# Loading two weight blocks by chunks of 32 rows into 128 partitions instead of by partition blocks of 32

## The chip, the cores and the metric

The kernel runs on one core of a Trainium2 chip. Its time is the device time of one execution, in microseconds (us). The engines are TensorE (PE; its weight loads are PEld), VectorE (DVE), ScalarE (ACT), GpSimd (POOL) and SyncE (SP). SP computes nothing here: it issues transfers, and ACT issues a few as well. All transfers are carried by the core's 16 DMA engines.

## The reference, cut to what matters

```python
h = jnp.maximum(_layernorm(x, axis=-1), 0.0)            # x: 128 graphs x 128 nodes x 768
q = _split_heads(h @ Wq + bq)                           # W: 768 x 768, 12 heads of 64
k = _split_heads(h @ Wk + bk)
v = _split_heads(h @ Wv + bv)
scores = jnp.einsum('bhqd,bhkd->bhqk', q, k) / 8 + beta * adj[:, None]
scores = jnp.where(adj[:, None] > 0, scores, -9e15)
out = x + (softmax(scores) @ v)                         # heads side by side again
```

Everything is float32.

## The kernel before, in words

The 128 graphs are worked on in 32 groups (G) of four (GRP). For each group three slices of projections are made: "qk0" (columns 0 to 383 of Wq and Wk), "v" (all of Wv) and "qk1" (columns 384 to 767 of Wq and Wk). The order is qk0, v, qk1, and the attention of a group is woven into the slices that follow.

From group 1 on, a slice is computed with sums of weight blocks (the tiles T_qk and T_v) in place of the weights themselves, line 557 (`product_z`). These sums are made once, during group 0, by DVE and POOL (`prepare`, lines 281 to 304): 45 of them, of which 11 stay in SBUF (names res_...) and 34 are written to HBM (names kept_..., line 290) and read back for each group (line 339). A sum that is to be written to HBM is built in a tile named prep_..., of which there are five, and three more shared with the attention's tile "e"; the next sum in the same tile can begin when the store has landed.

Group 0 uses the raw weights. They lie in one large tile, sbig: the first RAW = 4608 elements of a partition hold Wq and Wk of qk0 (later those of qk1), the next 4608 hold Wv, and behind them lie the first rows of x, an identity and some constants. Each weight matrix has 768 rows, and the row that goes with partition p and chunk c (c = 0 to 5) is 192 a + 32 c + j, where p = 32 a + j; a = 0 to 3 is a block of 32 partitions. The matmuls of group 0 take two chunks at a time: step k = 0, 1, 2 of a product uses chunks 2k and 2k + 1.

The opening of the program runs as follows.

- Four transfers bring the first two graphs of x (line 204), two from SP and two from ACT.
- `raw_qk0(k)` brings chunks 2k and 2k + 1 of Wq and Wk: for k = 0 Wq from SP and Wk from ACT, then k = 1 from SP. `load_x(0, 1)` brings the other two graphs of group 0, in four transfers. Then come k = 2 and `raw_v()`, all from SP.
- Behind them SP issues bv_b (the bias of v for all partitions, line 876), adj of group 0 (line 488), x of group 1 (line 196, eight transfers), and then the stores of the prepared sums (line 290).
- PE starts with fillers and transposes (lines 927, 913) and then computes qk0 for the first two graphs (`first_row`, line 1065), in the order: k = 0 for graph 0, k = 0 for graph 1, k = 1, k = 2. Then follow qk0 for the other two graphs (`plain_slice`, line 849), the v slice (line 849; the bias is added by a matmul with bv_b, line 854, behind k = 0 of each of its six products) and qk1.

The instructions of each engine and of each queue run in the order of the program. Each transfer counts up one of eight semaphores, taken in turn, and before a transfer is issued its queue waits for the one that used the same semaphore before it. So a queue has to wait for the landing of the transfer eight places earlier, counted over both queues.

One transfer elsewhere in the kernel has a source of the kind that the change introduces: `block` is filled in all 128 partitions from a small table of 32 rows in HBM that is read four times (lines 438 and 439). It happens once per group from group 2 on.

```python
later(lambda: nc.sync.dma_start(to.rearrange("p b s g -> p (b s g)"),
                                turned.rearrange("i b s -> i (b s)")[None].to_broadcast([NB, SQ, NB * 2 * GRP])), then)
```

Of the kernel before, what the change touches and what calls it, by code (L numbers as in the profile page):

```python
# [17 lines left out]
P = 128  # L18
# [12 lines left out]
@with_exitstack  # L31
def kernel(
    ctx: ExitStack,
    tc: tile.TileContext,
    x: bass.AP,
    adj: bass.AP,
    wq: bass.AP,
    bq: bass.AP,
    wk: bass.AP,
    bk: bass.AP,  # L40
    wv: bass.AP,
    bv: bass.AP,
    beta: bass.AP,
    out: bass.AP,
):

    nc = tc.nc
    keep = ctx.enter_context(tc.tile_pool(name="keep", bufs=1))
    bad = keep.tile([1, 1], I32, name="bad")
    args = (x, adj, wq, bq, wk, bk, wv, bv, beta, out)
    direct(tc, *args, bad)
    again = nc.values_load(bad[0:1, 0:1])
    with tc.If(again > 0):
        general(tc, *args)
# [69 lines left out]
def direct(ctx, tc, x, adj, wq, bq, wk, bk, wv, bv, beta, out, bad):  # L129
# [10 lines left out]
    nc = tc.nc  # L140
    B, N, D = x.shape
    HD = D // HEADS
    NC = D // P
# [6 lines left out]
    SQ = 32  # L150
    NB = P // SQ
# [21 lines left out]
    def flat(lo, hi):  # L173
        return sbig[:, lo:hi]
# [25 lines left out]
    for g in range(2):  # L200
        t = xg[0, g]
# [19 lines left out]

    wt = {}

    rows_of = {}
    for name, w in (("q", wq), ("k", wk), ("v", wv)):
        rows_of[name] = w.rearrange("(a c j) n -> a j c n", a=NB, j=SQ)

    def name_raw(u, v):
        for k in range(3):
# [2 lines left out]

    qk0_raw = flat(0, RAW).rearrange("p (c i j n) -> p c i j n", c=NC, i=2, j=3)

    def load_rows(engine, t, name, cols, chunks, order=range(NB)):
        for a in order:
            engine.dma_start(t[a * SQ:(a + 1) * SQ], rows_of[name][a][:, chunks, cols])

    def raw_qk0(k, engines=(nc.sync, nc.sync)):

        c = slice(2 * k, 2 * k + 2)
        for i, name in enumerate(("q", "k")):
            load_rows(engines[i], qk0_raw[:, c, i].rearrange("p c j n -> p c (j n)"), name, slice(0, 3 * P), c,
                      ((0, 1, 2, 3), (2, 3, 0, 1))[i])

    def raw_qk1_piece(at):
        v = flat(0, RAW).rearrange("p (c i n) -> p c i n", c=NC, i=2)
# [4 lines left out]

    def raw_v():
        t = flat(RAW, 2 * RAW).rearrange("p (c n) -> p c n", c=NC)
        load_rows(nc.sync, t, "v", slice(0, D), slice(0, NC))
        for k in range(3):
            for j in range(3):
                wt["v", f"B{k}{j}"] = t[:, 2 * k:2 * k + 2, j * 2 * P:(j + 1) * 2 * P].rearrange("p c (i n) -> p c i n", i=2)
# [75 lines left out]
    def load_T():  # L334
        if nt[0] < len(ring):
# [3 lines left out]
            nc.sync.dma_start(t, kept[sl, n])  # L339

    raw_qk0(0, (nc.sync, nc.scalar))
    raw_qk0(1)
    load_x(0, 1)
    raw_qk0(2)
    name_raw(0, qk0_raw)

# [526 lines left out]


    raw_v()
    nc.sync.dma_start(bv_b, bv[None, :].to_broadcast([P, D]))
    turned[0, "raw"] = load_adj(0)
# [455 lines left out]
```

## Time and profile before

| what | value |
|---|---|
| time, median of 3 runs (lowest to highest) | 2679.64 us (2677.68 to 2682.68) |
| the profiled execution: its own time | 2679.08 us |
| its span, from the first to the last instruction | 2677.2 us |
| granted TensorE clock | 0.998 |
| PE busy | 2652.1 us, 99% of the span |
| DVE, POOL, ACT busy | 81%, 77%, 65% |
| DMA: moved, mean rate | 721.70 MB, 270 GB/s |

The span is cut by the profile into rows of several views. In the timeline a row gives the start in us, the time taken, the engine ("SPq" and "ACTq" are the queues that issue transfers), the line of the kernel, and what is written from what, and in brackets the idle time before it with what ended it. In a table by windows, the columns are the busy time of each engine, the granted clock, the mean busy share of the 16 DMA engines and the GB/s that they moved; the share can go a little above 1. Durations come from the profiled execution, whose own time is 0.56 us under the median of the runs, less than the runs differ among themselves.

### The profile page before, as it was taken

What the parts mean: (1) busy time and instruction counts of PE and PEld (TensorE: products, weight loads), DVE (VectorE), ACT (ScalarE), POOL (GpSimd) and SP (SyncE); (2) the same over time, 40 slices, a digit from 0 to 9 for tenths busy, and PEclk for the clock granted to TensorE, in tenths of its full rate; (3) what the DMA queues carried; (4) which work ended last, traced back from release to release, by engine and by line L of the source; (5) the groups of instructions that cost most, each with busy time, mean ns of one, the idle gap of its engine ahead of it and who ended that gap; (6) DMA issues with size and microseconds to landing.
All of it is one profiled execution on the core that took longest, in us unless ns stands there. A gap on an engine that the chain in (4) does not pass through costs nothing.

```text
span 2677.2 us, 121501 instructions
## 1 busy us (share of the span) xinstructions
PE 2652.1 (99%) x52041; PEld 2563.4 (96%) x52041; DVE 2179.3 (81%) x2701; ACT 1747.9 (65%) x4608; POOL 2070.9 (77%) x3043
## 2 busy tenths in 40 slices
PE   9999999999999999999999999999999999999998
PEld 8799999999999999999999999999999999999997
DVE  7877888778888778888788887788887888887885
ACT  2567766676666677666766666776667676667654
POOL 5877778877778777788777787777887777887774
PEclk9999999999999999999999999999999999999999
DMA  8889888889888998889898888988898988898875
GB/s 252 270 273 282 272 268 277 270 269 282 277 271 272 266 287 265 276 275 277 265 282 279 269 273 273 283 272 272 276 280 264 280 278 271 274 278 272 260 239 159
DMA packets 526436, 721.70 MB, mean 270 GB/s; under 512 B 105916, under 2 KB 370120, under 8 KB 525896
## 3 DMA queue, kind: packets, MB, share of 16 engines
q1 hardware_dynamic: 525248, 713.12, 86.5%
q8 instruction: 411, 6.73, 1.0%
q14 instruction: 129, 1.06, 0.1%
q10 hardware_dynamic: 648, 0.79, 0.1%
HBM read 647.73 MB, written 66.05 MB: 267 GB/s over the span
## 4 chain that ended last, share of the span: by engine, by line
PE 39%; POOL 33%; ACT 13%; issue 6%; DMA 4%; DVE 4%; SPq 0%; POOLq 0%; ACTq 0%; DVEq 0%
PE pair L557 33%; POOL v L614 4%; PE pair L693 4%; POOL A L479 3%; POOL v L613 3%; POOL home L612 3%; PE pair L636 3%; ACT x L448 3%; ACT e L646 3%; POOL home L599 2%; POOL home L601 2%; ACT home L575 2%; ACT home L577 2%; POOL v L610 2%; POOL home L611 2%
## 5 line engine op out<-in xcount | busy, mean ns | idle before, releaser
L581 DVE TENSOR_TENSOR home<-home,pair 128x896 f32<-128x896 f32 x810 | 860.8, 1076 | 274.1 <-PE pair L557 217.4
L557 PE MATMUL pair<-sbig,T_qk 128*64 128x128 f32 x13020 | 832.9, 273 | 1.7 <-DVE sbig L474 0.8
L557 PEld LDWEIGHTS pair<-sbig,T_qk 128*64 128x64 f32 x13020 | 708.4, 137 | 11.4 <-issue 6.6
L557 PE MATMUL pair<-A,T_qk 128*64 128x128 f32 x6944 | 465.3, 273 | 0.0
L599 POOL TENSOR_TENSOR home<-home 128x256 f32<-128x256 f32 x298 | 246.6, 827 | 269.2 <-DVE home L581 261.6
L676 ACT ACTIVATE e<-e,sm 128x64 f32<-128x64 f32 x1512 | 382.3, 347 | 108.7 <-DVE sm L664 108.7
L557 PE MATMUL pair<-T_v,sbig 128*64 128x128 f32 x6944 | 415.4, 274 | 0.0
L693 PE MATMUL pair<-v,e 128*64 128x65 f32 x6048 | 401.6, 221 | 5.8 <-DVE e L644 5.7
L575 ACT ACTIVATE home<-pair 128x640 f32<-128x640 f32 x325 | 232.3, 715 | 262.4 <-PE pair L557 201.8
L557 PEld LDWEIGHTS pair<-T_v,sbig 128*64 128x64 f32 x6944 | 380.9, 137 | 12.3 <-issue 10.5
L557 PEld LDWEIGHTS pair<-A,T_qk 128*64 128x64 f32 x6944 | 377.4, 137 | 4.8 <-ACT e L705 4.4
L693 PEld LDWEIGHTS pair<-v,e 128*64 128x64 f32 x6048 | 356.2, 137 | 15.8 <-DVE e L644 12.8
L557 PE MATMUL pair<-sbig,res_qk 128*64 128x128 f32 x4340 | 288.4, 273 | 0.0
L602 POOL TENSOR_TENSOR home<-home 128x256 f32<-128x256 f32 x298 | 239.1, 802 | 23.4
L600 POOL TENSOR_TENSOR home<-home 128x256 f32<-128x256 f32 x298 | 229.2, 769 | 23.4
L557 PEld LDWEIGHTS pair<-sbig,res_qk 128*64 128x64 f32 x4340 | 234.6, 137 | 5.3 <-issue 5.3
L703 ACT ACTIVATE sm<-pair,tiny 128x8 f32<-128x8 f32 x189 | 49.5, 262 | 284.8 <-PE pair L693 284.7
L448 ACT ACTIVATE x<-x,block 128x192 f32<-128x192 f32 x480 | 232.6, 556 | 0.0
L601 POOL TENSOR_TENSOR home<-home 128x128 f32<-128x128 f32 x298 | 213.2, 715 | 23.4
L644 DVE SCALAR_TENSOR_TENSOR e<-pair,biasT 128x1024 f32<-128x1024 f32 x189 | 225.2, 1216 | 4.6 <-PE pair L636 4.6
L646 ACT ACTIVATE e<-e 128x1024 f32<-128x1024 f32 x189 | 194.0, 1068 | 52.6 <-DVE e L644 48.6
L479 POOL TENSOR_TENSOR A<-A 128x256 f32<-128x256 f32 x186 | 169.2, 910 | 57.0 <-DVE A L469 57.0
(204 smaller groups left out, 4595.7 us busy)
## 6 DMA issues: line engine op xcount, KB each, us to landing
T_qk<-kept_qk SPq DMA_DIRECT2D x713, 448.0 KB, 5.0
T_v<-kept_v SPq DMA_DIRECT2D x341, 448.0 KB, 4.3
xo<-in_x_dram SPq DMA_DIRECT2D x189, 256.0 KB, 5.0
out_dram<-xo SPq DMA_DIRECT2D x189, 256.0 KB, 6.2
x<-in_x_dram SPq DMA_DIRECT2D x248, 192.0 KB, 6.5
sbig<-in_x_dram SPq DMA_DIRECT2D x116, 384.0 KB, 6.4
kept_qk<-prep_qk SPq DMA_DIRECT2D x23, 448.0 KB, 3.3
adj<-in_adj_dram SPq DMA_DIRECT2D x128, 64.0 KB, 3.0
```

Of the source, the lines that this page charges most:

```text
L448: nc.scalar.activation(t, t, AF.Relu, bias=shift[G, n], scale=rstd[G, n])
L479: e.tensor_tensor(t[:, 0:2], t[:, 7:8].to_broadcast([P, 2, P]), t[:, 5:7], ALU.subtract)
L557: nc.tensor.matmul(p[q:q + HD, at, :], lhs[:, q:q + HD], rhs, start=(first and at % 4 == 0), stop=True, skip_group_check=True)
L575: nc.scalar.activation(t[:, 0:5], p[:, 0:5], AF.Copy, scale=float(sign))
L581: nc.vector.tensor_tensor(t, t, p[:, 0:7], op)
L599: e.tensor_tensor(t[:, 1:4:2], t[:, 1:4:2], twice(5), ALU.add)
L600: e.tensor_tensor(t[:, 2:5:2], t[:, 2:5:2], twice(1), ALU.add)
L601: e.tensor_tensor(t[:, 4], t[:, 4], t[:, 6], ALU.add)
L602: e.tensor_tensor(t[:, 0:7:6], t[:, 0:7:6], twice(2), ALU.add)
L646: trailing.append(lambda: nc.scalar.activation(e, e, AF.Exp, scale=1.0 / ISCALE))
L676: nc.scalar.activation(o[:, r, b, 0:HD], pa[:, r, b, 0:HD], AF.Copy, scale=t[:, 1, r, b:b + 1])
L693: nc.tensor.matmul(pa[q:q + HD, 2 * g + i, :], k[:, q:q + HD], vt[G, "v", r, h // 4][:, 4 * g + h % 4, :], start=True, stop=True, skip_gro ...
```

## The change

Each transfer now carries one chunk into all 128 partitions, where it carried two chunks (for Wv six) into 32 partitions. For qk0, 24 transfers of 96 KB become 12 of 192 KB; for v, 4 of 576 KB become 6 of 384 KB. The rows that are copied, their length (1536 B for qk0, 3072 B for v) and their places in sbig are the same. The source of a transfer was a list of 32 rows by two (six) chunks, and is now a list of 4 blocks by 32 rows; the destination was 32 partitions, and is now 128.

```diff
-    rows_of = {}
+    rows_of, whole_of = {}, {}
     for name, w in (("q", wq), ("k", wk), ("v", wv)):
-        rows_of[name] = w.rearrange("(a c j) n -> a j c n", a=NB, j=SQ)
+        whole_of[name] = rows_of[name] = w.rearrange("(a c j) n -> a j c n", a=NB, j=SQ)
...
-    def load_rows(engine, t, name, cols, chunks, order=range(NB)):
-        for a in order:
-            engine.dma_start(t[a * SQ:(a + 1) * SQ], rows_of[name][a][:, chunks, cols])
+    def load_chunk(engine, t, name, cols, c):
+        engine.dma_start(t, whole_of[name][:, :, c, cols])
 
     def raw_qk0(k, engines=(nc.sync, nc.sync)):
 
-        c = slice(2 * k, 2 * k + 2)
-        for i, name in enumerate(("q", "k")):
-            load_rows(engines[i], qk0_raw[:, c, i].rearrange("p c j n -> p c (j n)"), name, slice(0, 3 * P), c,
-                      ((0, 1, 2, 3), (2, 3, 0, 1))[i])
+        for c in (2 * k, 2 * k + 1):
+            for i, name in enumerate(("q", "k")):
+                load_chunk(engines[i], qk0_raw[:, c, i].rearrange("p j n -> p (j n)"), name, slice(0, 3 * P), c)
...
     def raw_v():
         t = flat(RAW, 2 * RAW).rearrange("p (c n) -> p c n", c=NC)
-        load_rows(nc.sync, t, "v", slice(0, D), slice(0, NC))
+        for c in range(NC):
+            load_chunk(nc.sync, t[:, c], "v", slice(0, D), c)
```

On PE the order of the instructions does not change. On SP, the opening of the queue stood as follows (partitions x chunks x elements; DMAHW0 to DMAHW7 are the eight semaphores):

```order
L204 DMA sbig<-in_x_dram 64x768 x2
L237 DMA sbig<-in_L_gnn_Wq_dram 32x2x384 x8
L237 DMA sbig<-in_L_gnn_Wk_dram 32x2x384 x4
L196 DMA x_1_129<-in_x_dram 32x8x192 x4
L237 DMA sbig<-in_L_gnn_Wq_dram 32x2x384 x4
L237 DMA sbig<-in_L_gnn_Wk_dram 32x2x384 x4
L237 DMA sbig<-in_L_gnn_Wv_dram 32x6x768 x4
L876 DMA bv_b<-in_L_gnn_bv_dram 128x768
```

and stands now:

```order
L204 DMA sbig<-in_x_dram 64x768 x2
L236 DMA sbig<-in_L_gnn_Wq_dram 128x1x384 x3
L236 DMA sbig<-in_L_gnn_Wk_dram 128x1x384
L236 DMA sbig<-in_L_gnn_Wq_dram 128x1x384
L236 DMA sbig<-in_L_gnn_Wk_dram 128x1x384
L196 DMA x_1_121<-in_x_dram 32x8x192 x4
L236 DMA sbig<-in_L_gnn_Wq_dram 128x1x384
L236 DMA sbig<-in_L_gnn_Wk_dram 128x1x384
L236 DMA sbig<-in_L_gnn_Wq_dram 128x1x384
L236 DMA sbig<-in_L_gnn_Wk_dram 128x1x384
L236 DMA sbig<-in_L_gnn_Wv_dram 128x1x768 x6
L875 DMA bv_b<-in_L_gnn_bv_dram 128x768
```

The weights' transfers kept their places between x and bv_b, and 20 of them on SP became 16. On ACT four transfers of Wk became two, and the three small loads behind the first Relu (line 935 to 937 before, 934 to 936 now) wait for other transfers. Before:

```order
L935 DMA beta_c<-in_L_gnn_beta_dram 128x1 [waits DMAHW2_49]
L936 DMA bqk_rows<-in_L_gnn_bq_dram 6x128 [waits DMAHW4_49]
L937 DMA bqk_rows<-in_L_gnn_bk_dram 6x128 [waits DMAHW5_49]
L919 ACTIVATE A_0_196<-pair_73 128x2x128 [waits PE_49]
L919 ACTIVATE A_0_202<-pair_73 128x2x128 [waits PE_49]
```

Now:

```order
L934 DMA beta_c<-in_L_gnn_beta_dram 128x1 [waits DMAHW0_49]
L935 DMA bqk_rows<-in_L_gnn_bq_dram 6x128 [waits DMAHW1_49]
L936 DMA bqk_rows<-in_L_gnn_bk_dram 6x128 [waits DMAHW2_49]
L918 ACTIVATE A_0_186<-pair_73 128x2x128 [waits PE_49]
L918 ACTIVATE A_0_192<-pair_73 128x2x128 [waits PE_49]
```

Before, they waited for one transfer of k = 0 and for the first two of the eight of k = 1; now they wait for the first three of the four of k = 1. The Relus behind them on ACT make the second graph's input for PE. On DVE one sum of v moved up by nine rows, ahead of sums of qk0 (names prep_qk_5 and prep_qk_12); it reads four of the six chunks of Wv. Now:

```order
L303 TENSOR_TENSOR prep_qk_10_410<-sbig 128x2x256
L303 TENSOR_TENSOR res_v_107<-sbig 128x2x256
L303 TENSOR_TENSOR prep_qk_5_412<-prep_qk_10_410,sbig 128x2x256
L280 TENSOR_TENSOR prep_qk_10_410<-prep_qk_10_410 128x128
L303 TENSOR_TENSOR prep_qk_12_420<-prep_qk_5_412,sbig 128x2x256
```

On POOL two copies of weights moved down by up to three rows.

## The prediction

> **What bounds the kernel now.** I read the page first, then who PE waits for in the first 110 us, then PE's timeline there, and last the queue, DVE and the DMA engines beside it. The page's first row says that TensorE is the bound:
>
> ```profile
> PE 2652.1 (99%) x52041; PEld 2563.4 (96%) x52041; DVE 2179.3 (81%) x2701; ACT 1747.9 (65%) x4608; POOL 2070.9 (77%) x3043
> ```
>
> The change touches only loads of the first 34 us, so what counts is whether PE gets its weights there. All its waits up to 110 us, and two windows:
>
> ```profile
> PE pair L927 <- POOL sbig masks.py:199: 1.5, 1, 1.5
> PE pair L373 <- DVE st L362: 1.3, 1, 1.3
> PE pair L849 <- ACT home L866: 0.4, 1, 0.4
> ...
> 0.00:30.00 30.00, 27.13 (x162) 24.34 (x163) 14.92 (x42) 7.69 (x19) 7.18 (x29) 1.00 0.86 206
> 30.00:100.00 70.00, 70.00 (x450) 54.47 (x453) 63.75 (x146) 23.98 (x53) 58.24 (x91) 1.00 0.89 292
> ```
>
> PE idles 2.87 us in the first 30 us, 1.5 of them before it has an identity, and not at all from 30 to 100. No wait names a weight. So quicker weights can win at most 2.87 - 1.5 = 1.4 us, while weights that come too late cost their whole delay, because no later idle time takes it up. When PE uses what:
>
> ```profile
> 9.05 1.06 PE L1065 MATMUL pair<-A,sbig 128*128 128x128 f32 x8
> 15.51 3.72 PE L1065 MATMUL pair<-A,sbig 128*128 128x256 f32 x16
> 22.91 5.45 PE L1065 MATMUL pair<-A,sbig 128*128 128x256 f32 x24
> 28.43 15.81 PE L849 MATMUL pair<-A,sbig 128*128 128x256 f32 x72
> 44.08 1.89 PE L849 MATMUL pair<-sbig,A 128*128 128x256 f32 x8
> 45.90 1.13 PE L854 MATMUL pair<-bv_b,ones 1*128 1x256 f32 x4
> 66.25 0.31 PE L373 MATMUL pair<-st,sbig 128*64 128x32 f32 x4
> 72.93 0.31 PE L387 MATMUL pair<-dev,sbig 128*64 128x32 f32 x4
> ```
>
> Chunks 0 and 1 of Wq and Wk are needed at 9.05, chunks 2 and 3 at 15.51, 4 and 5 at 22.91; Wv from 44.08, and bv_b at 45.90. The last two rows are the first places after that at which PE needs DVE's statistics of group 1. When they come, by the queues and by the landings:
>
> ```profile
> 2.00 6.88 SPq L237 DMA_DIRECT2D sbig<-in_L_gnn_Wq_dram  x8
> 18.39 2.17 SPq L237 DMA_DIRECT2D sbig<-in_L_gnn_Wv_dram  x4
> 20.61 0.61 SPq L876 DMA_DIRECT2D bv_b<-in_L_gnn_bv_dram  x1
> ...
> bv_b<-in_L_gnn_bv_dram SPq DMA_DIRECT2D x1, 384.0 KB, 13.2
> ```
>
> bv_b, the last transfer behind the weights, lands at 20.6 + 13.2 = 33.8, so it is 12.1 us early for PE. That is the cover of the whole opening.
>
> **How many DMA engines carry a transfer.** This decides the case, and the kernel has one transfer of the new kind, block<-turned: 128 partitions, from a list of 4 by 32 rows, here of 128 B. The end of its landing, in 40 slices of 10 ns from 2493.90 to 2494.30:
>
> ```profile
> GB/s 0 0 358 0 358 0 0 0 13 13 371 26 371 13 13 13 13 371 13 13 13 13 13 13 13 13 13 26 13 371 371 13 13 13 13 13 13 371 359 358
> DMA packets 44, 0.04 MB, mean 100 GB/s; under 512 B 34, under 2 KB 34, under 8 KB 44
> ...
> block<-turned SPq DMA_DIRECT2D x30, 16.0 KB
> ```
>
> 13 GB/s for 10 ns is one row of 128 B. From slice 9 to 38 each slice has one, two of them have two (26), and 358 more stands for a row of 3584 B of another transfer that begins: 32 rows of 128 B in a chain of 0.30 us, 9.4 ns apart. 32 is 128 divided by 4. Had 16 engines shared the rows, each would have 8. I read it as one engine's share of a transfer that only four engines carry, one for each of the four blocks of its source list, this one being late because it was still at other work. The eighteen new transfers have the same two lists, 4 by 32 rows into 128 partitions, so I take four engines for each. Whether always the same four, a trace without the engine's name can't tell; I take that too, and price the other case below.
>
> [...]
>
> **What an engine delivers.** Four windows, with share and GB/s at the end of each row:
>
> ```profile
> 4.50:10.00 5.50, 5.50 (x40) 5.34 (x39) 4.14 (x13) 2.34 (x5) 1.36 (x8) 1.00 0.87 239
> 14.00:19.00 5.00, 5.00 (x30) 4.32 (x29) 2.30 (x6) 0.17 (x1) 0.20 (x1) 1.00 0.88 227
> 22.00:31.00 9.00, 8.92 (x44) 7.29 (x43) 5.73 (x14) 4.03 (x10) 4.18 (x8) 1.00 1.04 209
> 40.00:50.00 10.00, 10.00 (x46) 8.29 (x45) 9.90 (x22) 0.84 (x2) 6.89 (x10) 1.00 1.00 378
> ```
>
> A busy engine moves GB/s / (16 x share): 17.2 and 16.1 with the weights of qk0, 12.6 with Wv into 32 partitions, 23.6 with stores from 128 partitions. These are the bounds of the unknown: 12.6 and 23.6. I take 17.2, that of the same 1536 B rows in the same place, which lies between.
>
> [...]
>
> **The sum.** Wq and Wk of qk0 are 12 x 196,608 B, or 589,824 B for each of four engines; Wv, 6 x 393,216 B, the same again. x of the other two graphs (four of 196,608 B) and bv_b (393,216 B) still go over all 16: 49,152 and 24,576 B for each. At 17.2 GB/s that is 11.4 us for each k, 34.3 for Wv, 2.9 and 1.4. Beginning at 4.5 us:
> - k = 0 lands at 15.9 (needed at 9.05), k = 1 at 27.4 (15.51), x at 30.2, k = 2 at 41.6 (22.91), Wv at 75.9, bv_b at 77.4 (before: 33.8).
> - PE does k = 2 in 5.45 us and the other two graphs in 15.81: the v slice begins at 62.9 instead of 44.08, and its first 1.89 us end at 64.8. Then it needs bv_b, so it waits until 77.4. Against 45.90 that is 31.5 us late.
> - Behind bv_b the queue is later still: 77.4 - 33.8 = 43.6 us, since the cover of 12.1 is gone. x of group 1 and the stores come next on SP, and DVE waits for both. In order of time:
>
> ```profile
> 44.62 1.12 DVE L362 BATCH_NORM_STATS2 st<-x 128x6 f32<-128x192 f32 x4
> 45.67 3.12 DVE L304 TENSOR_TENSOR prep_qk<-prep_qk,sbig 128x512 f32<-128x512 f32 x4
> 56.70 1.12 DVE L362 BATCH_NORM_STATS2 st<-sbig 128x6 f32<-128x192 f32 x4
> 67.94 0.20 DVE L380 SCALAR_TENSOR_TENSOR dev<-st,dev 128x32 f32<-128x32 f32 x1
> ...
> DVE prep_qk L304 <- DMA kept_qk<-prep_qk: 0.2, 1, 0.2
> ```
>
> The wait of 0.2 for a store says that DVE runs right behind the stores there, so it moves by the full 43.6. Its statistics then end at 57.8 + 43.6 = 101.4 for a PE that comes at 66.25 + 31.5 = 97.8, and the next step at 68.1 + 43.6 = 111.7 for a PE that comes at 72.93 + 35.1 = 108.0. Both are late, and PE ends 43.6 - (72.93 - 68.14) = 38.8 us behind.
>
> What costs nothing:
> - **Issuing.** Transfers of the new kind take longer to issue (0.54 us against 0.43):
>
> ```profile
> L438 SPq DMA_DIRECT2D block<-turned x30: 536/543/560, 112.1 to 2490.8; - x30
> L237 SPq DMA_DIRECT2D sbig<-in_L_gnn_Wq_dram x12: 312/426/1507, 2.0 to 16.0; - x12
> ```
>
>   On SP 16 x 0.54 = 8.7 us stand for 20 x 0.43 = 8.5, and SP now waits for landings, which covers both. With eight transfers in flight the four engines do not run dry.
> - **ACT's added wait.** beta, bq and bk now wait for three chunks of k = 1, up to about 27, and the Relus of the second graph stand behind them. PE needs these for at most the 6.5 us from 9.05 to 15.51, and then does k = 1, as long as k = 2: about 39. k = 2 lands at 41.6, which hides it; without that cover it would cost its own few us.
> - **DVE's moved sum** reads chunks 0 to 3 of Wv, here at 41.6 + 22.9 = 64.5, and would come by about 50. DVE then stands some 15 us, but it would stand for x of group 1 until after 77 in any case.
> - **Steady state.** Nothing is changed; what is lost stays.
>
> So the span grows by 38.8 us; 2679.64 + 38.8 = 2718 us. At 23.6 GB/s bv_b lands at 57.6, and PE is 11.7 late by bv_b and 19.0 by DVE; at 12.6, bv_b at 104, PE 66 by DVE and 70.5 if DVE's lead of 4.8 goes as well. The ends are +11.7 and +70.5: 2691 and 2750.
>
> **The rivals.** The bound for a change that can be told from none is 0.2%, 5.4 us.
> - The change does what it says: all 16 engines carry each transfer, or different fours in turn, which comes to the same. Then the weights' 4.72 MB take 12.5 us at 378 GB/s in place of 20.8 at 227, and PE wins its 1.4 us: 2678. For it speaks that 209 GB/s for Wv into 32 partitions is low beside 378; against it the chain of 32 rows. It decides from about nine engines on: 2,359,296 B / 9 + 49,152 in the 18.4 us up to 22.91 is 16.9 GB/s each, which they can give.
> - Four engines, fast: 23.6 GB/s, with little lost behind bv_b: 2691 to 2699. For it: 128 partitions on the other side. Four engines can't be hidden altogether, since k = 2 by 22.91 would ask for 639 KB in 18.4 us, 34.7 GB/s.
> - Four engines, slow: they hinder each other as in Wv's window: 2745 to 2750. For it: that window is the one with a queue that is never empty, which the new one is too.
> - The backlog isn't worked off: behind the weights the share was already 0.89 up to 100 us, so group 1 stalls again, at 2760 or more. Against it: between 100 and 110 us the share is 0.48 with 165 GB/s,
>
> ```profile
> 100.00:110.00 10.00, 9.62 (x130) 6.53 (x122) 10.00 (x17) 4.73 (x10) 8.94 (x15) 1.00 0.48 165
> ```
>
>   and while PE stands it asks for nothing new.
>
> **How the numbers follow.** Four engines at a middling rate, 2700 to 2745: 0.52. Fast: 0.19. Slow: 0.16. Backlog: 0.05. Sixteen or turns: 0.08, of which 0.06 within 0.2% and 0.02 faster. The predicted time is the first's, 2718; 2691 to 2750 leaves out the backlog, the last case and a little at both ends, about 0.16. Slower: 0.92.
>
> **What would show it.** In the changed kernel's profile: PE waiting in line 1064 for Wq or Wk, three times, and in line 853 for bv_b; a DMA share near 0.25 in the first 15 us, at 50 to 95 GB/s; bv_b landing 50 to 100 us into the span; then DVE waiting for x and stores and PE for DVE in lines 372 and 386, and every later group as long as before. A share near 0.9 with 300 GB/s or more in the opening, and PE without new waits, would make it wrong; so would 4 to 8 us of issue on SP for each transfer.

## The result, and the profile after

The changed kernel takes 2707.57 us (median of 4 runs, 2706.91 to 2708.22) against 2680.02 us (median of 4): a ratio of 1.0102, 95% interval 1.0085 to 1.0120, so slower by 27.6 us. The profiled execution took 2707.67 us, with a span of 2705.7, which is 28.5 more than the span before. In the changed kernel the line numbers behind the edit are one lower (L1064 was L1065, L848 was L849).

The page's row of busy times after:

```profile
PE 2662.1 (98%) x52041; PEld 2570.3 (95%) x52041; DVE 2180.6 (81%) x2701; ACT 1746.8 (65%) x4608; POOL 2069.4 (76%) x3043
```

PE has the same 52,041 instructions and is 10.0 us longer busy with them. The other 18.5 us are idle time. PE's waits in the first 160 us after (columns as in the prediction: us in total, times, longest):

```profile
PE pair L912 <- ACT A L918: 5.1, 1, 5.1
PE pair L848 <- ACT home L865: 4.9, 1, 4.9
PE pair L1064 <- DMA sbig<-in_L_gnn_Wq_dram: 3.7, 2, 3.4
PE pair L386 <- DVE dev L379: 3.5, 1, 3.5
PE pair L926 <- POOL sbig masks.py:199: 1.5, 1, 1.5
PE pair L853 <- DMA bv_b<-in_L_gnn_bv_dram: 1.3, 1, 1.3
PE pair L372 <- DVE st L361: 0.8, 1, 0.8
...
PE pair L1064 <- DMA sbig<-in_L_gnn_Wk_dram: 0.2, 1, 0.2
```

Before, PE waited for the identity (1.5 us), for DVE's first statistics (1.3) and for ACT's copy (0.4). Now it waits for Wq and Wk, for ACT's Relus (the first row), for bv_b, and later for DVE and for ACT's copy. Windows of the changed kernel (PEclk, DMA share and GB/s at the end of each row):

```profile
35.00:40.00 5.00, 5.00 (x27) 4.43 (x27) 2.45 (x8) 2.25 (x6) 4.10 (x8) 1.00 0.26 104
60.00:70.00 10.00, 10.00 (x37) 7.71 (x37) 1.14 (x4) 0.58 (x1) 0.00 (x0) 0.83 1.04 285
```

A share of 0.26 is four of 16 engines. They move 104 / (16 x 0.26) = 25.0 GB/s each, where the opening before had 17.2. Only when x and bv_b come, around 60 us, is the share full again.

PE's timeline after, at the places that the prediction used and at two behind them:

```profile
13.43 0.92 PE L1064 MATMUL pair<-A,sbig 128*128 128x128 f32 x4 [3.35 <-DMA sbig<-in_L_gnn_Wq_dram]
...
40.66 15.81 PE L848 MATMUL pair<-A,sbig 128*128 128x256 f32 x72
...
59.52 1.12 PE L853 MATMUL pair<-bv_b,ones 1*128 1x256 f32 x4 [1.32 <-DMA bv_b<-in_L_gnn_bv_dram]
60.57 7.13 PE L848 MATMUL pair<-sbig,A 128*128 128x256 f32 x24
...
82.42 0.31 PE L372 MATMUL pair<-st,sbig 128*64 128x32 f32 x4 [0.79 <-DVE st L361]
...
92.64 0.43 PE L386 MATMUL pair<-dev,sbig 128*64 128x32 f32 x4 [3.47 <-DVE dev L379]
93.00 6.77 PE L848 MATMUL pair<-sbig,A 128*128 128x256 f32 x24
...
128.58 6.39 PE L848 MATMUL pair<-A,sbig 128*64 128x256 f32 x36 [4.86 <-ACT home L865]
134.81 0.40 PE L692 MATMUL pair<-v,e 128*64 128x65 f32 x8
```

The last two places in the kernel before:

```profile
102.95 4.11 PE L849 MATMUL pair<-A,sbig 128*64 128x256 f32 x36 [0.39 <-ACT home L866]
106.89 0.40 PE L693 MATMUL pair<-v,e 128*64 128x65 f32 x8
```

From these rows and those of the prediction, how late PE is:

| place | before | after | late by |
|---|---|---|---|
| second row of qk0 | 28.43 | 40.66 | 12.2 |
| bv_b | 45.90 | 59.52 | 13.6 |
| L372 (statistics, first) | 66.25 | 82.42 | 16.2 |
| L386 (statistics, second) | 72.93 | 92.64 | 19.7 |
| second row of qk1 | 102.95 | 128.58 | 25.6 |
| behind its 36 multiplications | 106.89 | 134.81 | 27.9 |
| end of the span | 2677.2 | 2705.7 | 28.5 |

Nearly everything is lost in the first 135 us; the remaining 2,570 us add 0.6 in this profile. (In the profiles of the kernels below, the same stretch adds between -3.1 us, in e10, and +4.8, in e3, so 0.6 can't be told from nothing.) Two kinds of row add up here: waits, and groups that take longer than before with the same work, such as the 24 multiplications in 7.13 and 6.77 us in place of 5.45, and the 36 in 6.39 in place of 4.11. Over that last wait and group the granted clock is half:

```profile
126.40:133.30 6.90, 4.72 (x23) 2.66 (x24) 6.90 (x13) 3.21 (x7) 5.66 (x10) 0.51 0.62 200
```

DVE's timeline after, at the steps that the prediction moved:

```profile
64.68 1.14 DVE L361 BATCH_NORM_STATS2 st<-x 128x6 f32<-128x192 f32 x4 [7.93 <-DMA x<-in_x_dram]
70.09 3.14 DVE L303 TENSOR_TENSOR prep_qk<-prep_qk,sbig 128x512 f32<-128x512 f32 x4 [4.27 <-DMA kept_qk<-prep_qk]
81.14 1.13 DVE L361 BATCH_NORM_STATS2 st<-sbig 128x6 f32<-128x192 f32 x4
92.39 0.20 DVE L379 SCALAR_TENSOR_TENSOR dev<-st,dev 128x32 f32<-128x32 f32 x1
```

Against 44.62, 45.67, 56.70 and 67.94 before, these are late by 20.1, 24.4, 24.4 and 24.5 us: first by x of group 1, then by a store behind it on the queue.

### The profile page after: what moved, and what is told of

Same layout as the page of the kernel before. It is cut to its first block, busy times and chain, and to the rows that moved or that the text cites. A ratio compares the mean times of both kernels' runs of the same rounds, so it can differ in the third digit from the quotient of the medians.

```text
span 2705.7 us, 121473 instructions
## 1 busy us (share of the span) xinstructions
PE 2662.1 (98%) x52041; PEld 2570.3 (95%) x52041; DVE 2180.6 (81%) x2701; ACT 1746.8 (65%) x4608; POOL 2069.4 (76%) x3043
## 3 DMA queue, kind: packets, MB, share of 16 engines
q14 instruction: 129, 1.06, 0.1%
## 4 chain that ended last, share of the span: by engine, by line
PE 48%; POOL 19%; ACT 15%; DMA 9%; issue 5%; DVE 3%; SPq 1%; POOLq 0%; ACTq 0%; DVEq 0%
PE pair L556 39%; PE pair L692 4%; ACT x L447 3%; ACT e L645 3%; ACT home L574 3%; PE pair L635 2%; ACT home L576 2%; POOL v L613 2%; POOL home L598 2%; DMA turned<-row 2%; ACT e L675 2%; POOL home L600 2%; POOL v L612 2%; POOL A L478 2%; POOL home L611 2%
## 5 line engine op out<-in xcount | busy, mean ns | idle before, releaser
L692 PEld LDWEIGHTS pair<-v,e 128*64 128x64 f32 x6048 | 355.1, 137 | 16.5 <-DVE e L643 13.4
```

The source lines that it names most:

```text
L692: nc.tensor.matmul(pa[q:q + HD, 2 * g + i, :], k[:, q:q + HD], vt[G, "v", r, h // 4][:, 4 * g + h % 4, :], start=True, stop=True, skip_gro ...
```

## The experiments

Times are medians; each ratio is against runs of the kernel before on the same chip, whose medians were 2680.09 us (e1 to e4), 2680.22 (e5 to e8) and 2678.33 (e9, e10).

**Is it the number of blocks in the source list?** Three kernels with the changed kernel's instructions, in which only the list that a chunk is read from differs, so that W's rows come to other partitions:

```diff
-        whole_of[name] = rows_of[name] = w.rearrange("(a c j) n -> a j c n", a=NB, j=SQ)
+        rows_of[name] = w.rearrange("(a c j) n -> a j c n", a=NB, j=SQ)
+        whole_of[name] = w.rearrange("(b c j) n -> b j c n", b=16, j=8)
```

and the same with b=8, j=16 and b=2, j=64. In the expectations, theory E is that the number of blocks in this list sets the number of engines that carry a transfer, and that too few engines are the whole loss. The instructions that moved on DVE and POOL stand in them where the changed kernel has them.

> The rows of Wq, Wk (first slice) and Wv are dealt to the partitions as 16 blocks of 8 rows in place of 4 blocks of 32. The transfers keep their number, sizes, 128 partitions, order and two-level source list; the weights then meet other features than in the reference, so the output differs from it. [...] Here 16: bv_b lands before 34 us, PE has no new wait, 2677 to 2681 us. Theory L (list): a two-level source list into 128 partitions is slow as such, whatever its outer count: as the changed kernel, 2705 to 2710 us.

> As with 16 blocks, but 8 blocks of 16 rows; the output differs from the reference for the same reason. Theory E: eight engines at the 25 GB/s each that the changed kernel showed move 663,552 B each by 4.5 + 27 = 32 us, no later than before the change, so 2678 to 2683 us. Theory L: 2705 to 2710 us.

> The new transfers from a list of 2 blocks of 64 rows; W's rows come to other partitions, so the output is not the reference's, while every instruction is the changed kernel's. Theory E (the number of blocks is the number of engines, each at the 24 to 25 GB/s that the changed kernel shows): two engines, 49 GB/s in the opening; Wq and Wk of qk0 and Wv are 1,179,648 B each on an engine, 48 us and 48 us from about 4.5 us on, so bv_b lands near 105 instead of 57; DVE's chain, which goes with the queue, is 73 us behind the kernel before, and the time is 2745 to 2760. Rival L (a longer list, 64 rows for an engine, costs nothing more; the four of the changed kernel is a limit of the chip, not the block count): as the changed kernel, 2705 to 2710. Rival P (engines hinder each other at one side of the memory, and two do not): more than 25 GB/s for each, bv_b by 80, 2725 to 2735.

Measured: 2678.54 us with 16 blocks (ratio 0.9994, 0.9985 to 1.0004), 2685.59 with 8 (1.0027, 1.0017 to 1.0036), 2752.95 with 2 (1.0272, 1.0256 to 1.0288). Sixteen blocks give no loss and no gain that could be told; with two, PE waited 23.7 us for bv_b, until 103.6, where 105 was forecast. The pages' rows on packets, in the order before, 16 blocks, 8, 4 (the changed kernel) and 2:

```profile
DMA packets 526436, 721.70 MB, mean 270 GB/s; under 512 B 105916, under 2 KB 370120, under 8 KB 525896
```
```profile
DMA packets 526276, 721.70 MB, mean 269 GB/s; under 512 B 105756, under 2 KB 369960, under 8 KB 525736
```
```profile
DMA packets 526132, 721.70 MB, mean 269 GB/s; under 512 B 105612, under 2 KB 369816, under 8 KB 525592
```
```profile
DMA packets 526060, 721.70 MB, mean 267 GB/s; under 512 B 105540, under 2 KB 369744, under 8 KB 525520
```
```profile
DMA packets 526024, 721.70 MB, mean 263 GB/s; under 512 B 105504, under 2 KB 369708, under 8 KB 525484
```

All have the same bytes. Against before, 160, 304, 376 and 412 small packets are missing. No row shows which transfer a small packet belongs to. If each transfer has one on each engine that carries it, 28 old transfers on 16 engines had 448, and 18 new ones on k engines have 18k: 448 - 18k is 160, 304, 376 and 412 for k = 16, 8, 4 and 2, exactly. So by this count the number of blocks of this source list was the number of engines, at 16, 8, 4 and 2. Windows of the kernels with 16, 8 and 2 blocks, in which weights are loaded, say the same by their share (third figure from the end is PEclk, then share and GB/s):

```profile
15.00:30.00 15.00, 14.83 (x78) 12.26 (x78) 7.80 (x24) 4.20 (x11) 4.75 (x11) 1.00 1.02 250
```
```profile
5.00:10.00 5.00, 4.41 (x32) 4.03 (x30) 3.77 (x12) 1.84 (x5) 1.36 (x8) 1.00 0.55 179
```
```profile
5.00:10.00 5.00, 3.73 (x30) 3.34 (x28) 3.96 (x13) 1.67 (x5) 1.36 (x8) 1.00 0.15 51
```

Divided by the number of engines, two move 51 / 2 = 25.5 GB/s each, four 104 / 4 = 26.0, eight 179 / 8 = 22.4 and sixteen 250 / 16 = 15.6 (the last two windows hold some transfers of other kinds as well). So four did not hinder each other, and in these loads the rate of one engine was lower with sixteen at work, with 128 partitions (15.6) as with 32 (17.2, 16.1 and 12.6 in the kernel before). What limits the sixteen no run here shows.

The kernel with 8 blocks missed its expectation. PE's first waits in it, all but the one for the identity:

```profile
PE pair L913 <- ACT A L919: 3.6, 1, 3.6
...
PE pair L1065 <- DMA sbig<-in_L_gnn_Wk_dram: 0.9, 1, 0.9
PE pair L1065 <- DMA sbig<-in_L_gnn_Wq_dram: 0.5, 1, 0.5
```

The weights are only 1.4 us late, but the Relus stand on ACT behind beta, bq and bk, which wait for chunks of k = 1. PE began the second row of qk0 at 34.18, 5.8 late. The prediction had that wait down as hidden by k = 2; here nothing hides it.

**Is it ACT's added wait?** In the changed kernel, and in the one with 8 blocks, the three small loads were issued right behind Wk of k = 0:

```diff
     raw_qk0(0, (nc.sync, nc.scalar))
...
+    nc.scalar.dma_start(beta_c, beta[None, :].to_broadcast([P, 1]))
+    nc.scalar.dma_start(bqk_rows[0:NC], bq.rearrange("(c p) -> c p", p=P))
+    nc.scalar.dma_start(bqk_rows[NC:2 * NC], bk.rearrange("(c p) -> c p", p=P))
...
-    with tc.issue_after(first["relu"].ins):
-        nc.scalar.dma_start(beta_c, beta[None, :].to_broadcast([P, 1]))
...
```

> The changed kernel, with beta, bq and bk issued on ACT right behind Wk of k = 0 and not behind the first Relus. Theory A (their wait for a semaphore of k = 1 holds ACT's Relus of the second graph for 12.8 us, and PE 5.1 of it): PE's wait of 5.1 us for A in line 912 goes to below 1; but k = 2 still lands at about 34, so PE waits for Wq or Wk there instead, the first row ends no more than 2 us earlier, and behind it DVE's chain sets the end: 2705 to 2708, no change. Rival B (the wait is PE's own loss and carries to the end): 5 us less, 2702 to 2703.

> The kernel with 8 blocks of 16 rows (output not the reference's), with beta, bq and bk moved in the same way. With 8 blocks the weights were only 1.4 us late, yet row 1 of qk0 began 5.75 us late, behind PE's wait of 3.6 for A in line 913 and half a clock for 3.4 us. Theory A (the small loads' wait on ACT): the wait in line 913 goes, row 1 begins 1 to 2.5 us late instead of 5.75, and the time is 2680 to 2682, against 2685.6. Rival B (eight engines are the cause, and the wait only shows where it is felt): PE waits for Wq and Wk instead, row 1 begins 4 us or more late, and the time stays at 2684 to 2687.

Measured: 2708.70 us (1.0109, 1.0094 to 1.0125; 0.7 above the forecast of no change) and 2686.06 us (1.0024, 1.0014 to 1.0033). In e6 the wait of 5.1 in line 912 is gone, the second row of qk0 begins at 38.38, 2.3 earlier than in the changed kernel (2 at most were forecast), and the time is the same. In e7 the wait of 3.6 is gone, the second row begins at 32.14, 3.7 late (between the two forecasts), and no gain shows in the time against 8 blocks alone. In both, part of the wait has only moved. PE's timeline in e6 has a new wait for the first Relus:

```profile
12.33 0.80 PE L1063 MATMUL pair<-A,sbig 128*128 128x128 f32 x2 [3.03 <-ACT A L921]
```

ACT's timeline in e7 shows the reason: bk's issue now ends at 8.75 us, and the first Relus (line 922), at 8.01 in e2, stand behind it:

```profile
8.48 0.27 ACTq L348 DMA_DIRECT2D bqk_rows<-in_L_gnn_bk_dram  x1
...
10.19 0.91 ACT L922 ACTIVATE A<-pair 128x256 f32<-128x256 f32 x3
```

So in the changed kernel the 2.3 us that PE won at the second row of qk0 are worth nothing. With 8 blocks the cause of the loss stays open in part: PE is 5.7 us late behind the second row of qk1 in e2 (112.58 against 106.89), and in e7 it would be 3.3, its 3.7 less the 0.4 that the kernel before waits for ACT's copy and e7 does not, but the times, 5.5 and 5.8 above the kernel before, do not show this difference.

**Which half of the change?** One kernel keeps the change for Wq and Wk alone, the other for Wv alone:

```diff
 e3: raw_v as before
-        for c in range(NC):
-            load_chunk(nc.sync, t[:, c], "v", slice(0, D), c)
+        for a in range(NB):
+            nc.sync.dma_start(t[a * SQ:(a + 1) * SQ], rows_of["v"][a])
```

```diff
 e4: raw_qk0 as before
-                load_chunk(engines[i], qk0_raw[:, c, i].rearrange("p j n -> p (j n)"), name, slice(0, 3 * P), c)
...
+            for a in ((0, 1, 2, 3), (2, 3, 0, 1))[i]:
+                engines[i].dma_start(t[a * SQ:(a + 1) * SQ], rows_of[name][a][:, c, 0:3 * P])
```

> Only Wq and Wk are loaded by chunks; Wv as before the change. Theory C (chain): the end is late by as much as bv_b and the stores behind it land late, since DVE follows the stores and PE follows DVE without slack, plus 2 to 3 us in which the clock is halved after waits. bv_b lands near 47 instead of 33.8: 13 + 2 to 3, so 2695 us. Theory S (slack): PE is late by its own weights (12 us) and keeps some 5 us of lead on DVE: 2692 to 2693 us.

> Only Wv is loaded by chunks; Wq and Wk as before the change. PE gets bv_b at about 45, just in time (45.9). Theory C (chain): everything behind bv_b is 11 us later, and so is the end, plus 2 us of halved clock: 2692 to 2694 us. Theory S (slack): 5 to 8 us of lead are used up first: 2683 to 2687 us. If the two parts simply add up, this and the kernel with Wq and Wk alone lose 27.5 us together.

Measured: 2700.03 us (1.0074, 1.0054 to 1.0094) and 2696.57 us (1.0063, 1.0046 to 1.0080): 19.9 and 16.5 us, together more than the 27.6 of both. Both times lie above every forecast made for them (2692 to 2695 and 2683 to 2694). In e3 the loss is PE's own and lies ahead of the second row of qk0:

```profile
40.81 5.84 PE L1064 MATMUL pair<-A,sbig 128*128 128x256 f32 x18 [3.18 <-DMA sbig<-in_L_gnn_Wk_dram]
46.49 3.83 PE L848 MATMUL pair<-A,sbig 128*128 128x256 f32 x17
```

That is 18.1 late, 5.8 later than in the changed kernel, where the second theory had taken 12. The DMA share there is 0.99 from 30 to 45 us, as Wv spreads over all engines again. I read it so that the four which still carry Wk of k = 2 have Wv's rows to do too. Behind it PE has no new wait. In e4 the opening is as before and the loss is DVE's chain, seen in the same three waits behind bv_b as in the changed kernel:

```profile
PE pair L850 <- ACT home L867: 4.8, 1, 4.8
PE pair L374 <- DVE st L363: 3.8, 2, 2.4
PE pair L388 <- DVE dev L381: 3.5, 1, 3.5
```

PE is 1.3 late at bv_b, 14.2 behind the last of these waits (117.19 against 102.95) and 17.0 behind the 36 multiplications that follow, which take 6.90 us in place of 4.11. I read it so that the halves don't add because PE's lateness ahead of bv_b and DVE's behind it run side by side, and the later one counts.

**Is it PE's lateness or DVE's chain that reaches the end?** In e10 bv_b is issued ahead of Wv; in e9 15 multiplications of the identity stand ahead of PE's wait for DVE's dev:

```diff
 e10
+    nc.sync.dma_start(bv_b, bv[None, :].to_broadcast([P, D]))
     raw_v()
-    nc.sync.dma_start(bv_b, bv[None, :].to_broadcast([P, D]))
```

```diff
 e9: moments_2
         n = hi - lo
+        for _ in range(15 * (G == 1)):
+            nc.tensor.matmul(pm[G, lo, "bank"][:, 1, 0:P], ident, ident, start=True, stop=True)
```

> The changed kernel, with bv_b issued ahead of Wv and not behind it. Theory C (DVE's chain): bv_b has landed when PE asks for it, so PE's wait of 1.3 us in line 853 and the half clock behind it go, and PE stands 2 to 3 us longer for DVE in lines 372 and 386; x of group 1 and the stores come behind the same transfers as before, so the end and the time stay, 2706 to 2710. Rival P (PE's lateness at bv_b, which the prediction took for one of the two bounds, carries to the end): 1.3 to 3 us less, 2704 to 2706.

> The changed kernel, with 15 multiplications of the identity (3.4 us at full clock) ahead of PE's wait of 3.5 us for DVE's dev in line 386, in free columns of that bank. Theory C (behind bv_b it is DVE's chain that sets the end, so what PE loses between two of its waits for that chain costs nothing): no half clock at 92 to 96 us, the 24 multiplications behind take 5.45 us and not 6.77, qk1 begins 1.3 us earlier, and PE's wait for ACT's copy in line 848 grows from 4.9 to about 6.2; the end and the time stay, 2707 to 2709. Rival S (what PE loses at the half clock there stays to the end): the wait stays at 4.9, and the time is 1.3 us less, 2706.

Measured for e10: 2705.30 us (1.0096, 1.0079 to 1.0113), an interval that holds the changed kernel's 1.0102. The time by itself lies in rival P's band, 0.7 below the other one; but the kernel before was 1.7 faster here as well, and against it e10 is 27.0 us slower, the changed kernel 27.6. So the trace decides. In PE's timeline PE does not wait for bv_b, waits longer for DVE instead (5.9 us in lines 372 and 386 against 4.3, 1.6 more where 2 to 3 were expected), and is at the same point in time where it waits for ACT's copy, 128.41 against 128.58:

```profile
57.55 1.13 PE L853 MATMUL pair<-bv_b,ones 1*128 1x256 f32 x4
...
81.86 0.43 PE L372 MATMUL pair<-st,sbig 128*64 128x32 f32 x4 [3.88 <-DVE st L361]
...
128.41 6.24 PE L848 MATMUL pair<-A,sbig 128*64 128x256 f32 x36 [5.22 <-ACT home L865]
```

e9 did something else than meant. The added multiplications themselves waited, for DVE's read of the same bank, and so ran behind the wait and not in it:

```profile
92.17 5.24 PE L386 MATMUL pair<-sbig 128*128 128x128 f32 x30 [2.72 <-DVE mean L375]
97.35 0.31 PE L388 MATMUL pair<-dev,sbig 128*64 128x32 f32 x4
...
129.20 5.79 PE L850 MATMUL pair<-A,sbig 128*64 128x256 f32 x36 [2.22 <-ACT home L867]
```

They made PE 4.7 us late at dev (97.35 against 92.64) and 3.3 at the start of qk1 (107.67 against 104.41). Yet the wait for ACT's copy shrank from 4.9 to 2.2, its end moved by 0.6, and the time is 2708.48 us (1.0107, 1.0090 to 1.0123): the same. What it was to say of the half clock it doesn't say, but it shows that 3 us of PE's time just ahead of that wait are worth nothing.

**Does the half clock cost?** In e8 20 multiplications of the identity stand ahead of the last wait, in columns that nothing else reads:

```diff
 e8: plain_slice
+                    if sl == "qk1" and n == 8:
+                        for _ in range(20):
+                            nc.tensor.matmul(bank[:, 0, H2:H2 + P], ident, ident, start=True, stop=True)
```

> The changed kernel, with 20 matrix multiplications of the identity (4.5 us at full clock) ahead of PE's wait of 4.9 us for ACT's copy in line 848, in free columns of the bank just computed. Theory H (the half clock behind a wait comes from PE standing idle, and its loss of 2.3 us at this place, behind DVE's chain, stays to the end): no window of half clock at 126 to 133 us, the next 36 multiplications take 4.1 us and not 6.4, and PE is 25.6 to 26.5 us late from there on instead of 27.9; the time is 2705 to 2706. Rival K (the half clock comes from something else, such as the transfers or the other engines at this place): the windows stay, and the time is 2707 to 2709. The times alone can hardly tell the two apart; the clock and PE's timeline do.

Measured: 2705.34 us (1.0095, 1.0079 to 1.0110). The clock is full there and the 36 multiplications take 4.11 us again, though PE still waits 1.27:

```profile
126.50:133.30 6.80, 5.53 (x51) 4.11 (x52) 6.80 (x13) 3.22 (x7) 4.30 (x7) 1.00 0.49 144
```
```profile
129.44 4.11 PE L848 MATMUL pair<-A,sbig 128*64 128x256 f32 x36 [1.27 <-ACT home L868]
133.38 0.40 PE L692 MATMUL pair<-v,e 128*64 128x65 f32 x8
```

PE is 133.38 - 106.89 = 26.5 late there against 27.9, within the forecast. 1.4 us are won, not 2.3, since the wait ended 0.9 later in this run. The times alone don't tell it from the changed kernel; the trace does.

## Why the prediction was right or wrong

Slower was right, and 2707.6 lies in the range, 10 us below the 2718 that stood as likeliest.

- **Four engines for each transfer:** right, and now counted (376 packets). That they are the same four is shown by the share of 0.26 with many transfers under way: different fours in turn would have filled it.
- **What an engine delivers:** this term was mis-sized. Taken at 17.2 GB/s, it measured 25.0 by the share in the cleanest window, beyond the upper bound of 23.6. From 4.5 us to bv_b's end at 59.5, all the bytes that the prediction counted for an engine (2 x 589,824 + 49,152 + 24,576) went at 22.8 GB/s, gaps included. The landings followed: Wv's first four chunks let DVE go on at 51.14 where 64.5 was forecast, and bv_b came at 59.5 and not at 77.4. The row taken was one with all 16 engines at work, and that is where the step went wrong: the kernel with 16 blocks, which has the changed kernel's rows and 128 partitions, moves 250 / (16 x 1.02) = 15.3 by the same reckoning. So 128 partitions did not make an engine fast by themselves (15.3); with only four at work it was (25.0). The row of 23.6 lay nearer by luck: it was one of stores, on all 16.
- **The waits ahead of bv_b:** the prediction had one for each of k = 0, 1 and 2. The three that came, 3.9 us in all, are those for k = 0; for k = 1 and 2 PE did not wait, and it began k = 2 at 35.18 where 41.6 was forecast. Of the 12.2 us at the second row of qk0, the rest is the 5.1 for ACT's Relus and about 4 at half clock, less the 1.3 for DVE's first statistics, for which PE no longer waits.
- **bv_b and DVE:** the places were right, each of them. PE waited in line 853 for bv_b, then for DVE in lines 372 and 386, and DVE moved by 24.4, nearly bv_b's own 59.5 - 33.8 = 25.7. At line 386 PE was 19.7 late, which is that 24.5 less DVE's lead of 4.8, as the prediction's formula has it.
- **"PE ends 43.6 - (72.93 - 68.14)":** this step failed. The lead of 4.8 does not last to the end. At the second row of qk1 PE waits for ACT's copy (home), and ACT makes this copy behind a step that waits for DVE's bias (biasT). ACT's rows, before and after:

```profile
101.36 0.73 ACT L498 ACTIVATE adj<-adj,beta_s 128x512 f32<-128x512 f32 x1 [6.58 <-DVE biasT L497]
```
```profile
126.99 0.72 ACT L497 ACTIVATE adj<-adj,beta_s 128x512 f32<-128x512 f32 x1 [7.80 <-DVE biasT L496]
```

  This step is 25.6 late, as DVE, 24.5 late at dev, has by then lost another 1.2 in waits for a store and for POOL. The kernel before had already waited 0.4 us for the copy, so nothing was in hand: PE's 19.7 became 25.6. That wait stood among the three that the prediction quoted, and the sum stopped one wait short of it. The prediction had the case in its upper end alone.
- **What a wait costs behind itself:** the prediction had nothing for it. In the five stretches at half clock (listed at the end) PE is busy 19.3 us by the windows; half of that, 9.7, is about the 10.0 us by which PE's busy time grew. Most of that was swallowed by waits that followed, and 2.3 us (27.9 - 25.6) behind the last one reached the end. e8 won 1.4 of them back.
- So the measured sum is: 25.6 for DVE's chain, none of its lead given back, 2.3 for the clock, 0.6 later: 28.5. With bv_b at its measured 59.5, the prediction's own sum gives 59.5 - 33.8 - 4.8 = 20.9. So the rate alone made the forecast of 38.8 too long by 17.9, and what the sum left out, 7.6, took part of it back: that it came within 10 us is in part luck.
- **ACT's added wait, hidden by k = 2:** wrong in the reason, right in the price. ACT stood 12.8 us, PE 5.1 of them, and k = 2 did not make PE wait afterwards, so k = 2 hid it no longer. What hides it is DVE's chain: in e6 the second row of qk0 began 2.3 us earlier, and the time was the same. "Without that cover it would cost its own few us" fits e2, with 5.8 us at the second row; e7 showed that issuing the loads earlier doesn't mend it there, since the wait then comes at the first Relus.
- **Issuing, steady state:** right; the 0.6 us in the last 2,570 are less than profiles differ there.
- **The rivals.** Sixteen engines were priced at 2678, and the kernel with 16 blocks took 2678.5, but not by the way described: it moved 250 GB/s and not 378, its second row of qk0 began 0.2 us earlier and not 1.4, and the interval of its ratio holds 1. The turning point, "about nine engines", was worked out from k = 2. Eight do lose 5.5 us, but PE waits for k = 0 and for ACT there, and not for k = 2. Four fast engines were the case that came for the rate, but not for its 2691 to 2699, by the lead and the clock. Four that hinder each other: not seen, neither in e5 (25.5 GB/s for each of two) nor in the changed kernel (26.0 for each of four). The backlog was worked off: later groups stand where they stood, but for the 0.6 us.

Not tried was a version with x of group 1 ahead of Wv on the queue, so it stays open how much of DVE's 24.4 that alone would save.

## What to carry to other kernels

The outer dimension of a transfer's source list can decide how many DMA engines carry it: here four blocks left the DMA share at 0.26, though every transfer filled 128 partitions, and 16 blocks cost nothing, 8 cost 5.5 us, 4 cost 27.6 and 2 cost 73. So look at the DMA share and at the count of small packets as soon as a list is rewritten. And a delay is followed to the last place at which an engine waits in the profile of before, however short that wait is: a wait of 0.4 us says that there is no slack, and a lead counted ahead of it is gone.

## What the runs showed of the hardware that was not expected

- Around some of PE's waits its clock was half for 3.4 us, or twice that. In the changed kernel the granted clock was 0.50 from 13.8 to 17.2, 20.6 to 27.4, 61.6 to 65.0 and 92.3 to 95.7, and 0.51 from 126.4 to 133.3, each beginning within a wait or just behind one. The length of the wait alone doesn't decide it: 1.32 us at bv_b was followed by 7.13 us for 24 multiplications that otherwise take 5.45, while 2.44 us at the first statistics in e4 was followed by 24 in 5.45. In the rows shown here the multiplications behind every wait of 3 us or more were slower in this way (the shortest is 3.03, in e6, with two in 0.80 us behind it, where the kernel before has eight in 1.06). With e8's multiplications in the last wait the clock was 1.00 from 126.5 to 133.3. So PE's standing idle matters, the 1.32 us shows that a wait well short of 3.4 can be enough, and what else decides it no run here settles.
- What one engine moved in these loads went with how many were at work: with the new lists 25.5 GB/s with two, 26.0 with four, 22.4 with eight and 15.6 with sixteen, each by the GB/s of a window over the number of engines.
